# Layer 1's products on two column groups behind the sums over the values, with one shift in sixteen on GpSimd and a unit's last sums on TensorE

## The chip, the core and the metric

The kernel runs on one core of a Trainium2 chip. The metric is the device time of one execution in microseconds, lower is better. Before the change three executions took 4672.19, 4672.76 and 4673.68 us. A profiled execution, which all durations below come from, took 4667.5 us, with a span of 4665.7 us from the first to the last instruction and a mean granted TensorE clock of 0.997.

## The reference

The input x is two images of 256 channels and 64 x 64 = 4096 positions, in 32-bit floats. Two attention layers follow one another. Layer 0 normalises over the channels, has 4 heads of 16 channels, a gate and a sigmoid. The change leaves it alone. Layer 1 is this, with 4 heads of 64 channels:

```
qkv = einsum('oc,bchw->bohw', w_qkv, x) + b_qkv
q, k, v = split(qkv.reshape(b, 4, 3 * 64, 4096), 3, axis=2)
attn = softmax(einsum('bhdn,bhdm->bhnm', q, k) / 8, axis=-1)
out = einsum('bhnm,bhdm->bhnd', attn, v).reshape(b, 256, 64, 64)
return einsum('oc,bchw->bohw', w_out, out) + b_out + x
```

So for every image and head a matrix of 4096 x 4096 scores is formed, exponentials of it are taken, and it is multiplied with the values and divided by its row sums.

## The kernel before

**Units, groups, chunks and steps.** Layer 1 works in 32 units `(b, g, j)`: image b, pair of heads g, block j of 512 queries (eight blocks). A unit goes over the keys in 32 chunks of 128. A chunk is a tile of 128 keys x 2 heads x 512 queries, so 128 x 1024 numbers. The chunks of a unit fall into two groups of 16, each with its own maximum. The program is written as one loop over 16 steps a unit with two chunks a step, in the order in which each engine shall work (every instruction goes through `seq`, which keeps the order of the program on its engine). What belongs to a chunk is spread over several steps, with LAG = 11:

- `score(t)` (L865): for each of the two heads a product on TensorE of 64 rows x 128 columns, side by side on the two halves of the array's rows, into one of two "pair" buffers of PSUM (two banks each).
- `keep(t)` (L882): VectorE takes the running maximum of the group, `rmax` (L893); ScalarE copies the scores out of PSUM into a tile `raw` (L894). There are 26 `raw` buffers.
- At the end of a group, `turn_max` (L896) transposes the maxima on TensorE, once for each head, and `fold` (L911) reduces them on VectorE to the negated maximum of each query (L923). It is sent to memory and read back as a row, spread over all partitions (tile `row`, one buffer). `place_shift` (L939) copies the row to PSUM on ScalarE, in another order of its columns (L943).
- `shift(t)` (L949): 11 steps after its score, VectorE adds the negated maximum to the chunk (L951).
- `weigh(t)` (L958): ScalarE takes the exponential (L963); GpSimd adds the chunk to the group's running sum `acc` (L973 for a group's first two chunks, L975 for the others). In the last chunks of the last unit, TensorE does part of that work (`on_tensor`, `late_sums`).
- `gather(t)` (L996): TensorE multiplies the exponentials with the values and sums over the keys, for each head in one of two column groups of the array (128 rows x 64 columns, L1004). 16 chunks add up in PSUM; then ScalarE copies the sum out (L1015).
- After a unit: `total` (L1018) sums the two `acc` over the partitions on TensorE, in four column groups of 32 (L1026); `keep_total` copies them out (L1034) and sends them through memory, four stores and a load on SyncE's queue; `lose`, `add_sums`, `factors` join the two groups' sums (small operations on GpSimd, a reciprocal on VectorE, L1124); `turn_sums` (L1128, with `turned`, L1048) transposes the gathered sums, and `rows` (L1131) scales them on VectorE (L1135) and joins them on GpSimd (L1141, L1144).

**The products.** Next to this, TensorE makes the queries of the next unit, the keys and values for the unit eight units on, and in the last 8 units the output of the first image. Each is a block of 512 positions, cut into four quarters. `quarter` (L803) is a product of 128 rows x 128 columns over 256 positions (keys and queries, L806); `values_in` (L690) has two products of 128 rows x 128 columns over 128 columns of the weights (L693); `project_out` (L1156) is like a quarter (L1160). ScalarE copies the results out (`store_keys` L818, `store_values` L832, `keep_next_queries` L858, `output` L1170).

**The order.** `at(t, place, step)` hangs a piece of work on step t at a place. Within a step the loop at the end of the kernel runs in this order:

1. the scores of the step's two chunks; the exponential of the second chunk of the pair due one step before; pieces at "start"; pieces at "early";
2. `keep` of the first chunk; `shift` and `weigh` of the first chunk due now; pieces at "early end";
3. `keep` of the second chunk; `gather` of the two chunks of the pair due one step before; pieces at "late" and "late end";
4. `shift` of the second chunk due now; pieces at "end".

So on TensorE a piece "early" stands between the scores and the sums over the values (`gather`), and a piece "late" behind the sums and ahead of the next step's scores. On ScalarE "early end" stands ahead of the copy of the second chunk, and "start" behind the exponential and ahead of the copy of the first.

**PSUM.** Two "pair" buffers take four of the eight banks, the shifts two, `gather` one, and one bank called "misc" serves all else in turn: products, transposes and totals. Whoever wants "misc" waits until its last user was copied out.

Of the kernel before, what the change touches and what calls it, by code (L numbers as in the profile page):

```python
# [14 lines left out]
P = 128  # L15
# [11 lines left out]
def conv_attention_kernel(  # L27
# [738 lines left out]

    LATE = len(units) * NM - 2 * LAG
    with (
# [34 lines left out]
        def quarter(ps, xt, g, t, q):  # L803

            c, cols = q % 2, bass.ts(q // 2, NB // 2)
            seq(nc.tensor.matmul(  # L806
                ps[:, cols], w1[:, c, t, bass.ts(g, P)], xt[:, c, cols],
                start=(c == 0), stop=(c == CC - 1),
            ))

        def next_keys(b, g, i, q):
            if q == 0:
                halves_of["k"] = misc(f"k1p_{b}_{g}_{i}")
            quarter(halves_of["k"], loaded["kv", b, g, i], g, 1, q)
# [8 lines left out]
        def next_values(b, g, i, q):  # L823
            if q % 2 == 0:
                halves_of["vp"] = misc(f"v1p_{b}_{g}_{i}_{q}")
            values_in(halves_of["vp"], loaded["kv", b, g, i], g, q)
# [20 lines left out]
        def next_queries(u, q):  # L847
# [6 lines left out]
            quarter(halves_of["q"], loaded["q", u], g, 0, q)  # L854
# [84 lines left out]
        def place_shift(u, n):  # L939
# [7 lines left out]
            shifts[u, n] = ps  # L947

        def shift(t):  # L949
            u = units[t // NM]  # L950
            seq(nc.vector.tensor_tensor(  # L951
                raws[t], raws[t], shifts[u, t % NM // GS], ALU.add
            ))
# [4 lines left out]
        def weigh(t):  # L958
# [6 lines left out]
            if on_tensor(t):  # L965
                return
# [29 lines left out]
        def gather(t):  # L996
# [13 lines left out]
            elif t == 2 * END - 2:  # L1010
                late_sums((t, t + 1))
            raws.pop(t - 2, None)
# [5 lines left out]
        def total(u):  # L1018
# [3 lines left out]
            srows[u] = misc(f"sum1_{b}_{g}_{j}")  # L1022
            for n in range(NG):
                for k in range(2):
# [3 lines left out]
                        start=True, stop=True,  # L1028
# [127 lines left out]
        def project_out(b, j, o, q):  # L1156
            if q == 0 or o == 1 and q == 2:
                outs["ps"] = misc(f"o1_{b}_{j}_{o}_{q}")
            c, cols = q % 2, bass.ts(q // 2, NB // 2)
            seq(nc.tensor.matmul(  # L1160
                outs["ps"][:, cols], wo1[:, c, bass.ts(o, P)], loaded["ao", b, j][:, c, cols],
                start=(c == 0), stop=(c == CC - 1),
            ))
# [28 lines left out]

        for n, u in enumerate(units):
            b, g, j = u
            t0 = n * US
            if n > 0:
                at(t0 - 9, "start", lambda u=u, b=b, j=j: fetch(("q", u), x1[b][j]))
                for q in range(4):
                    at(t0 - (5, 5, 3, 2)[q], "early", lambda u=u, q=q: next_queries(u, q))
                at(t0 - 5, "early end", lambda u=u: keep_next_queries(u, 0))  # L1200
                at(t0 - 2, "early end", lambda u=u: keep_next_queries(u, 1))
            if n < len(units) - NJ:
                to = (*units[n + NJ][:2], j)
                at(max(t0 - 1, 0), "start", lambda to=to: fetch(("kv", *to), x1[to[0]][to[2]]))
                for q in range(4):
                    at(t0 + 2 + q, "early", lambda to=to, q=q: next_keys(*to, q))
                    at(t0 + (6, 7, 9, 10)[q], "early", lambda to=to, q=q: next_values(*to, q))
                at(t0 + 5, "early end", lambda to=to: store_keys(*to))
                for i, step in enumerate((t0 + 7, t0 + 10)):
                    at(step, "early end", lambda to=to, i=i: store_values(*to, i))  # L1210
# [12 lines left out]
            if u != units[-1]:  # L1223
                at(t1 + 4, "early", lambda u=u: total(u))
                at(t1 + 4, "early end", lambda u=u: keep_total(u))
                at(t1 + 1, "late", lambda u=u: lose(u))
                at(t1 + 5, "late end", lambda u=u: add_sums(u))
                at(t1 + 7, "start", lambda u=u: factors(u))
# [15 lines left out]
            if n >= len(units) - NJ:  # L1244
                b0 = B - 2
                at(t0 - 1, "start", lambda b0=b0, j=j: fetch_output(b0, j))
                for o in range(CC):
                    for q in range(4):
                        step = t0 + ((2, 3, 4, 5), (6, 7, 9, 10))[o][q]
                        at(step, "early", lambda b0=b0, j=j, o=o, q=q: project_out(b0, j, o, q))  # L1250
                at(t0 + 5, "early end", lambda b0=b0, j=j: output(b0, j, 0, 2))
                for part, step in enumerate((t0 + 7, t0 + 10)):
                    at(step, "early end", lambda b0=b0, j=j, part=part: output(b0, j, 1, part))
# [172 lines left out]
```

## Time and profile before

| | before |
|---|---|
| three executions, median | 4672.76 us |
| profiled execution: time, span | 4667.5 us, 4665.7 us |
| PE busy | 4496.5 us |
| DVE busy | 3894.2 us |
| ACT busy | 3429.5 us |
| POOL busy | 2513.9 us |
| layer 1's shift, L951 on DVE | 1024 times, 1209 ns each |
| layer 1's maximum, L893 on DVE | 960 times (and 32 first ones), 1217 ns each |
| GpSimd's sum, L975 and L973 on POOL | 883 times, 2373 ns each, and 64 times, 2385 ns each |
| scores, L876 on PE | 4096 records, 637 ns each |
| sums over the values, L1004 on PE | 4096 records, 605 ns each |
| totals, L1026 on PE | 248 records, 605 ns each |
| a quarter of a product, L806 on PE | records of 431 ns |

PE is TensorE's products, PEld its loads of weights, DVE VectorE, ACT ScalarE, POOL GpSimd, SP SyncE. A product in 32-bit floats leaves two records in the profile, and records of products that run side by side overlap; the busy time counts such time once. A line such as "L951 DVE ... xN | busy, mean" is a group of instructions of one line of the program. "x <- y: total, times, longest" in the table of waits says that x's engine stood idle until y was done. The timeline gives start, duration, engine, line and operation, with the idle time before it in brackets; like instructions that follow one another are drawn together (x8).

### The profile page before, as it was taken

The page shows a single profiled execution, that of the slowest core. Times are in us where ns is not written, and L with a number is a line of the kernel's source. Part 1 is how long each engine was busy: PE and PEld are TensorE (multiplying, and loading weights), DVE is VectorE, ACT ScalarE, POOL GpSimd, SP SyncE. Part 2 cuts the span into 40 slices and gives each one's busy share as a digit, 9 for nine tenths or more (in the row PEclk, how much of TensorE's full clock was granted, in tenths as well). Part 3 has the DMA queues.
Part 4 walks back from the last instruction along what each step waited for, and adds up shares of the span by engine and source line. Part 5 has one row for each costly group of instructions (what it writes and reads, how often), then busy time and mean ns, then how long its engine had stood idle before and what let it go on. Part 6 is the DMA issues. An engine that isn't in the chain of part 4 may idle for free. (4 is left out here: it accounts for less than half of the span.)

```text
span 4665.7 us, 70910 instructions
## 1 busy us (share of the span) xinstructions
PE 4496.5 (96%) x27290; PEld 1511.0 (32%) x27290; DVE 3894.2 (83%) x4506; ACT 3429.5 (74%) x4588; POOL 2513.9 (54%) x1306
## 2 busy tenths in 40 slices
PE   8999999999999999999999999999999999999998
PEld 3433333333333333332333333333333333222232
DVE  6777777777777777439999999999999999999997
ACT  3366666666666666668888888888888888888885
POOL 5300000000000000009999999999999999999995
PEclk9999999999999999999999999999999999999999
DMA  3100000000000000121111221111211112121213
GB/s 100 39 4 20 20 20 15 15 15 15 15 17 15 15 13 13 40 77 35 35 37 33 63 48 42 35 37 43 69 41 39 37 33 62 48 53 37 53 39 111
DMA packets 199682, 174.70 MB, mean 37 GB/s; under 512 B 121256, under 2 KB 122088, under 8 KB 199344
## 3 DMA queue, kind: packets, MB, share of 16 engines
q1 hardware_dynamic: 197488, 169.58, 13.9%
q8 instruction: 214, 3.51, 0.3%
q14 instruction: 124, 1.02, 0.1%
q10 hardware_dynamic: 1856, 0.59, 0.1%
HBM read 127.65 MB, written 42.48 MB: 36 GB/s over the span
## 5 line engine op out<-in xcount | busy, mean ns | idle before, releaser
L975 POOL TENSOR_TENSOR acc<-acc,raw 128x1024 f32<-128x1024 f32 x883 | 2095.2, 2373 | 82.3 <-ACT raw L963 21.1
L402 DVE TENSOR_REDUCE mx<-a 128x1 f32<-128x512 f32 x2048 | 1314.4, 685 | 449.7 <-PE a L398 448.7
L439 ACT ACTIVATE p<-s 128x512 f32<-128x512 f32 x2048 | 1107.8, 595 | 702.1 <-PE a L398 369.3
L876 PE MATMUL s<-q,k 64*128 64x512 f32 x4096 | 1120.9, 637 | 126.1 <-ACT raw L894 117.9
L951 DVE TENSOR_TENSOR raw<-raw,shift 128x1024 f32<-128x1024 f32 x1024 | 1234.2, 1209 | 3.9 <-ACT shift L943 2.6
L893 DVE TENSOR_TENSOR rmax<-s,rmax 128x1024 f32<-128x1024 f32 x960 | 1168.7, 1217 | 74.4 <-PE s L876 68.3
L436 PE MATMUL s<-q,kT 32*128 32x512 f32 x4096 | 1218.0, 640 | 0.0
L894 ACT COPY raw<-s 128x1024 f32<-128x1024 f32 x1024 | 1034.2, 1010 | 207.3 <-DVE rmax L893 162.0
L963 ACT ACTIVATE raw<-raw 128x1024 f32<-128x1024 f32 x1024 | 1084.8, 1060 | 133.6 <-DVE raw L951 101.2
L398 PE MATMUL a<-kT,q 32*128 32x512 f32 x4096 | 1129.3, 643 | 1.4 <-DVE mx L402 1.3
L1004 PE MATMUL av<-raw,v 128*64 128x512 f32 x4096 | 992.8, 605 | 3.5 <-ACT raw L963 3.4
L451 PE MATMUL av<-p,v 128*32 128x256 f32 (+1 forms) x7904 | 650.1, 399 | 0.6 <-ACT avs L465 0.6
L876 PEld LDWEIGHTS s<-q,k 64*128 64x128 f32 x4096 | 314.6, 185 | 858.5 <-ACT raw L894 600.9
L501 POOL TENSOR_TENSOR f<-f,dyn 128x16 f32<-128x16 f32 x15 | 3.3, 221 | 1027.3 <-DVE f L500 1027.3
L436 PEld LDWEIGHTS s<-q,kT 32*128 32x128 f32 x4096 | 397.2, 183 | 425.8 <-issue 392.6
L451 PEld LDWEIGHTS av<-p,v 128*32 128x32 f32 x7904 | 157.7, 108 | 751.4 <-issue 737.1
L1004 PEld LDWEIGHTS av<-raw,v 128*64 128x64 f32 x4096 | 247.7, 136 | 468.8 <-issue 350.1
L552 POOL TENSOR_SCALAR res<-res 128x1024 f32<-128x1024 f32 x16 | 16.7, 1045 | 659.6 <-ACT res L551 659.6
L398 PEld LDWEIGHTS a<-kT,q 32*128 32x128 f32 x4096 | 305.1, 183 | 31.5 <-DVE mx L402 18.2
L973 POOL TENSOR_TENSOR acc<-raw,raw 128x1024 f32<-128x1024 f32 x64 | 152.6, 2385 | 124.2 <-ACT raw L963 124.2
L923 DVE TENSOR_REDUCE negs<-rt 128x4 f32<-128x512 f32 x126 | 86.7, 688 | 50.4 <-PE rt L906 50.4
L306 DVE RECIPROCAL std<-std 128x128 f32<-128x128 f32 x64 | 56.1, 920 | 39.5 <-ACT std L301 39.5
(335 smaller groups left out, 1835.1 us busy)
## 6 DMA issues: line engine op xcount, KB each, us to landing
row<-neg SPq DMA_DIRECT2D x128, 256.0 KB
x<-in_x_dram SPq DMA_DIRECT2D x16, 512.0 KB
res<-in_x_dram SPq DMA_DIRECT2D x16, 512.0 KB
x<-res SPq DMA_DIRECT2D x16, 512.0 KB
att<-rows SPq DMA_DIRECT2D x62, 128.0 KB
kd<-k1s SPq DMA_DIRECT2D x24, 256.0 KB
vd<-v1s SPq DMA_DIRECT2D x24, 256.0 KB
k<-kd SPq DMA_DIRECT2D x24, 256.0 KB
```

Source lines behind the costliest of these rows:

```text
L398: seq(nc.tensor.matmul(ps, qs0[u][r, bass.ts(i, P)], kTs[b][r, bass.ts(m, NB)], start=True, stop=True,))
L402: seq(nc.vector.tensor_reduce(mxs[u][:, i * H + h, m : m + 1], ps, AX.X, ALU.max))
L436: seq(nc.tensor.matmul(ps, kTs[b][r, bass.ts(m, P)], qs0[u][r, :], start=True, stop=True))
L439: seq(nc.scalar.activation(pt[:, k, :], ps, AF.Exp, scale=D0**-0.5))
L451: seq(nc.tensor.matmul(avs[u][32 * h : 32 * h + 32, cols], vs0[b][:, m, 32 * h : 32 * h + 32], pts[t, h // 2][:, h % 2, cols], start=(m == ...
L876: seq(nc.tensor.matmul(ps[:, k, :], ks[b, g, m // PB][r, bass.ts(m % PB, P)], qs1[u][r, :], start=True, stop=True,))
L893: seq(nc.vector.tensor_tensor(rmax[u, n], ps, before, ALU.max))
L894: seq(nc.scalar.copy(raw, ps))
L951: seq(nc.vector.tensor_tensor(raws[t], raws[t], shifts[u, t % NM // GS], ALU.add))
L963: seq(nc.scalar.activation(p, p, AF.Exp, scale=D1**-0.5))
L975: seq(nc.gpsimd.tensor_tensor(accs[u, n], accs[u, n], p, ALU.add))
L1004: seq(nc.tensor.matmul(avs1[u, n][k * D1 : (k + 1) * D1, :], v[:, m % PB, k, :], raws[t][:, k, :], start=(m % GS == 0), stop=(m % GS == GS ...
```

## The change

Six things change, all in layer 1:

- `quarter` makes two products of 128 rows x 64 columns, one for each column group, in place of one of 128 x 128; so does `next_values` (its halves are 64 positions), and `project_out` now goes through `quarter`.
- These products, and `total`, hang "late" in place of "early". The copies of their results on ScalarE hang at the "start" of the next step in place of "early end" of the same. Two quarters of the queries move from step 11 to step 13, one from 13 to 14 (counted from the start of the unit before).
- For the chunk number 11 of each group (the twelfth), GpSimd adds the shift, straight from the tile `row`, right behind `place_shift`; VectorE leaves it out. The last group of the last unit keeps the old way.
- The last two chunks of each unit are no longer added to `acc` on GpSimd. Behind the last `gather` of a unit, TensorE sums them over the partitions, with four products of 128 x 32 columns into the bank of the total, and `total` adds the second group's `acc` onto them. So the "misc" bank belongs to the total from that step on.
- `add_sums` moves two steps later, and `factors` from the start of step 15 to the end of the step after.

```
--- before.py
+++ after.py
@@ -764,6 +764,9 @@
     END = len(units) * US
 
 
+    ALSO = 11
+
+
     LATE = len(units) * NM - 2 * LAG
     with (
         tc.tile_pool(name="l1", bufs=2) as l1,
@@ -800,18 +803,20 @@
 
 
 
-        def quarter(ps, xt, g, t, q):
+
+        def quarter(ps, xt, w, q):
 
             c, cols = q % 2, bass.ts(q // 2, NB // 2)
-            seq(nc.tensor.matmul(
-                ps[:, cols], w1[:, c, t, bass.ts(g, P)], xt[:, c, cols],
-                start=(c == 0), stop=(c == CC - 1),
-            ))
+            for k in range(2):
+                r = slice(k * D1, (k + 1) * D1)
+                seq(nc.tensor.matmul(
+                    ps[r, cols], w[:, c, r], xt[:, c, cols], start=(c == 0), stop=(c == CC - 1),
+                ))
 
         def next_keys(b, g, i, q):
             if q == 0:
                 halves_of["k"] = misc(f"k1p_{b}_{g}_{i}")
-            quarter(halves_of["k"], loaded["kv", b, g, i], g, 1, q)
+            quarter(halves_of["k"], loaded["kv", b, g, i], w1[:, :, 1, bass.ts(g, P)], q)
 
         def store_keys(b, g, i):
             k = l1.tile([P, NB], F32, tag="kv", name=f"k1s_{b}_{g}_{i}")
@@ -823,7 +828,14 @@
         def next_values(b, g, i, q):
             if q % 2 == 0:
                 halves_of["vp"] = misc(f"v1p_{b}_{g}_{i}_{q}")
-            values_in(halves_of["vp"], loaded["kv", b, g, i], g, q)
+            ps, xt = halves_of["vp"], loaded["kv", b, g, i]
+            for c in range(CC):
+                for k in range(2):
+                    r = slice(k * D1, (k + 1) * D1)
+                    seq(nc.tensor.matmul(
+                        ps[r, bass.ts(q, P)], xt[:, c, q * P + k * D1 : q * P + (k + 1) * D1],
+                        w1[:, c, 2, bass.ts(g, P)], start=(c == 0), stop=(c == CC - 1),
+                    ))
 
         def store_values(b, g, i, half):
             if half == 0:
@@ -851,7 +863,7 @@
                 qs1[u] = qt
             if q % 2 == 0:
                 halves_of["q"] = misc(f"q1p_{b}_{g}_{j}_{q}")
-            quarter(halves_of["q"], loaded["q", u], g, 0, q)
+            quarter(halves_of["q"], loaded["q", u], w1[:, :, 0, bass.ts(g, P)], q)
 
         def keep_next_queries(u, half):
             cols = bass.ts(half, NB // 2)
@@ -945,9 +957,19 @@
                 row.rearrange("p k (a m i) -> p (k a) i m", m=P, i=2),
             ))
             shifts[u, n] = ps
+            if (u, n) != (units[-1], NG - 1):
+                a = raws[units.index(u) * NM + n * GS + ALSO]
+                seq(nc.gpsimd.tensor_tensor(
+                    a.rearrange("p k (a i m) -> p (k a) i m", m=P, i=2),
+                    a.rearrange("p k (a i m) -> p (k a) i m", m=P, i=2),
+                    row.rearrange("p k (a m i) -> p (k a) i m", m=P, i=2),
+                    ALU.add,
+                ))
 
         def shift(t):
             u = units[t // NM]
+            if t % GS == ALSO and t < (len(units) - 1) * NM + GS:
+                return
             seq(nc.vector.tensor_tensor(
                 raws[t], raws[t], shifts[u, t % NM // GS], ALU.add
             ))
@@ -962,7 +984,7 @@
             p = raws[t]
             seq(nc.scalar.activation(p, p, AF.Exp, scale=D1**-0.5))
 
-            if on_tensor(t):
+            if on_tensor(t) or m >= NM - 2:
                 return
             if (u, n) not in first:
                 first[u, n] = p
@@ -1009,6 +1031,15 @@
                 late_sums((t - 1, t) if on_tensor(t - 1) else (None, t))
             elif t == 2 * END - 2:
                 late_sums((t, t + 1))
+            if m == NM - 1 and u != units[-1]:
+                srows[u] = misc(f"sum1_{b}_{g}_{j}")
+                for i in (t - 1, t):
+                    for k in range(2):
+                        r = D1 * (NG - 1) + 32 * k
+                        seq(nc.tensor.matmul(
+                            srows[u][r : r + 32, :], ones[:, :32], raws[i][:, k, :],
+                            start=(i < t), stop=False, skip_group_check=True,
+                        ))
             raws.pop(t - 2, None)
             if m % GS == GS - 1:
                 a = l1.tile([P, NB], F32, tag="avs", name=f"avs1_{b}_{g}_{j}_{n}")
@@ -1019,13 +1050,12 @@
 
 
             b, g, j = u
-            srows[u] = misc(f"sum1_{b}_{g}_{j}")
             for n in range(NG):
                 for k in range(2):
                     r = D1 * n + 32 * k
                     seq(nc.tensor.matmul(
                         srows[u][r : r + 32, :], ones[:, :32], accs[u, n][:, k, :],
-                        start=True, stop=True,
+                        start=(n < NG - 1), stop=True, skip_group_check=True,
                     ))
 
         def keep_total(u):
@@ -1156,11 +1186,7 @@
         def project_out(b, j, o, q):
             if q == 0 or o == 1 and q == 2:
                 outs["ps"] = misc(f"o1_{b}_{j}_{o}_{q}")
-            c, cols = q % 2, bass.ts(q // 2, NB // 2)
-            seq(nc.tensor.matmul(
-                outs["ps"][:, cols], wo1[:, c, bass.ts(o, P)], loaded["ao", b, j][:, c, cols],
-                start=(c == 0), stop=(c == CC - 1),
-            ))
+            quarter(outs["ps"], loaded["ao", b, j], wo1[:, :, bass.ts(o, P)], q)
 
         def output(b, j, o, part):
 
@@ -1190,24 +1216,25 @@
 
 
 
+
         for n, u in enumerate(units):
             b, g, j = u
             t0 = n * US
             if n > 0:
                 at(t0 - 9, "start", lambda u=u, b=b, j=j: fetch(("q", u), x1[b][j]))
                 for q in range(4):
-                    at(t0 - (5, 5, 3, 2)[q], "early", lambda u=u, q=q: next_queries(u, q))
-                at(t0 - 5, "early end", lambda u=u: keep_next_queries(u, 0))
-                at(t0 - 2, "early end", lambda u=u: keep_next_queries(u, 1))
+                    at(t0 - (3, 3, 2, 2)[q], "late", lambda u=u, q=q: next_queries(u, q))
+                at(t0 - 2, "start", lambda u=u: keep_next_queries(u, 0))
+                at(t0 - 1, "start", lambda u=u: keep_next_queries(u, 1))
             if n < len(units) - NJ:
                 to = (*units[n + NJ][:2], j)
                 at(max(t0 - 1, 0), "start", lambda to=to: fetch(("kv", *to), x1[to[0]][to[2]]))
                 for q in range(4):
-                    at(t0 + 2 + q, "early", lambda to=to, q=q: next_keys(*to, q))
-                    at(t0 + (6, 7, 9, 10)[q], "early", lambda to=to, q=q: next_values(*to, q))
-                at(t0 + 5, "early end", lambda to=to: store_keys(*to))
-                for i, step in enumerate((t0 + 7, t0 + 10)):
-                    at(step, "early end", lambda to=to, i=i: store_values(*to, i))
+                    at(t0 + 2 + q, "late", lambda to=to, q=q: next_keys(*to, q))
+                    at(t0 + (6, 7, 9, 10)[q], "late", lambda to=to, q=q: next_values(*to, q))
+                at(t0 + 6, "start", lambda to=to: store_keys(*to))
+                for i, step in enumerate((t0 + 8, t0 + 11)):
+                    at(step, "start", lambda to=to, i=i: store_values(*to, i))
 
                 t1 = (n // NJ * NJ + NJ - 1) * US
                 at(t1 + 2 * j + 2, "start", lambda to=to: load_keys(*to))
@@ -1221,11 +1248,11 @@
                 at(t1 + 2, "end", lambda u=u, k=k: place_shift(u, k))
             t1 = t0 + US + GS // 2
             if u != units[-1]:
-                at(t1 + 4, "early", lambda u=u: total(u))
-                at(t1 + 4, "early end", lambda u=u: keep_total(u))
+                at(t1 + 4, "late", lambda u=u: total(u))
+                at(t1 + 5, "start", lambda u=u: keep_total(u))
                 at(t1 + 1, "late", lambda u=u: lose(u))
-                at(t1 + 5, "late end", lambda u=u: add_sums(u))
-                at(t1 + 7, "start", lambda u=u: factors(u))
+                at(t1 + 7, "late end", lambda u=u: add_sums(u))
+                at(t1 + 8, "end", lambda u=u: factors(u))
                 for place, k in (("early", 1), ("late", 0)):
                     at(t1 + 9, place, lambda u=u, k=k: turn_sums(u, k))
                     at(t1 + 9, f"{place} end", lambda u=u, k=k: rows(u, k))
@@ -1247,10 +1274,10 @@
                 for o in range(CC):
                     for q in range(4):
                         step = t0 + ((2, 3, 4, 5), (6, 7, 9, 10))[o][q]
-                        at(step, "early", lambda b0=b0, j=j, o=o, q=q: project_out(b0, j, o, q))
-                at(t0 + 5, "early end", lambda b0=b0, j=j: output(b0, j, 0, 2))
-                for part, step in enumerate((t0 + 7, t0 + 10)):
-                    at(step, "early end", lambda b0=b0, j=j, part=part: output(b0, j, 1, part))
+                        at(step, "late", lambda b0=b0, j=j, o=o, q=q: project_out(b0, j, o, q))
+                at(t0 + 6, "start", lambda b0=b0, j=j: output(b0, j, 0, 2))
+                for part, step in enumerate((t0 + 8, t0 + 11)):
+                    at(step, "start", lambda b0=b0, j=j, part=part: output(b0, j, 1, part))
```

## The prediction

> **What bounds the kernel now.** I read the page first: does one engine bound the whole span? Its second view has PE at nine tenths everywhere, and DVE, ACT and POOL jump near the middle, where layer 1 begins. The page's totals mix two layers; the change touches layer 1 only, so I read 2500 to 4500 us of the table by windows (columns: PE, PEld, DVE, ACT, POOL busy).
>
> ```profile
> span 4665.7 us, 70910 instructions
> PE 4496.5 (96%) x27290; PEld 1511.0 (32%) x27290; DVE 3894.2 (83%) x4506; ACT 3429.5 (74%) x4588; POOL 2513.9 (54%) x1306
> ...
> 2500.00:4500.00 2000.00, 1897.26 (x7960) 613.92 (x7956) 1902.10 (x1753) 1741.69 (x1881) 1875.65 (x916) 1.00 0.19 46
> ```
>
> Three engines are at 94 to 95%, so none alone says what a step costs. The waits of the same stretch say who waits for whom:
>
> ```profile
> ACT raw L894 <- DVE rmax L893: 119.5, 202, 1.0
> PE s L876 <- ACT raw L894: 86.8, 174, 0.9
> POOL acc L973 <- ACT raw L963: 64.5, 51, 2.1
> DVE rmax L893 <- PE s L876: 52.1, 125, 0.6
> ```
>
> This is a ring: scores (PE), maximum (DVE), copy out of PSUM (ACT), next scores into the two freed "pair" buffers. The copies L1034, one per unit, stand 79.8 us apart (2182.1 to 4577.7 in 30 intervals: 79.85). I call a unit's 16 steps 0 to 15 and walk through one in the timeline. PE, steps 7 to 9 and 11 to 13:
>
> ```profile
> 3034.99 1.13 PE L876 MATMUL s<-q,k 64*128 64x512 f32 x4
> 3036.41 1.13 PE L876 MATMUL s<-q,k 64*128 64x512 f32 x4 [0.29 <-ACT raw L894]
> 3037.47 0.66 PE L906 MATMUL rt<-ident,rmax 128*128 128x128 f32 x4
> 3038.05 1.94 PE L1004 MATMUL av<-raw,v 128*64 128x512 f32 x8
> 3039.92 0.66 PE L906 MATMUL rt<-ident,rmax 128*128 128x128 f32 x4
> 3040.51 2.14 PE L876 MATMUL s<-q,k 64*128 64x512 f32 x8
> ...
> 3052.59 1.13 PE L806 MATMUL q1p<-b_('q', (0, 1, 5))_25110,w 128*128 128x256 f32 x4
> 3053.66 1.94 PE L1004 MATMUL av<-raw,v 128*64 128x512 f32 x8
> 3055.52 2.38 PE L876 MATMUL s<-q,k 64*128 64x512 f32 x8
> 3057.84 1.06 PE L1026 MATMUL sum<-acc,ones 128*32 128x512 f32 x8
> 3058.83 1.94 PE L1004 MATMUL av<-raw,v 128*64 128x512 f32 x8
> 3060.70 2.15 PE L876 MATMUL s<-q,k 64*128 64x512 f32 x8
> 3062.78 0.70 PE L806 MATMUL q1p<-b_('q', (0, 1, 5))_25110,w 128*128 128x256 f32 x2
> 3063.41 1.94 PE L1004 MATMUL av<-raw,v 128*64 128x512 f32 x8
> ```
>
> Starts count, since ends overlap. The second score waits for a copy; then everything follows in order. av takes 1.87 us, one product 0.63 (3062.78 to 3063.41), two in one go 1.07, so 0.44 each and 0.19 once for coming from and going to another shape. DVE spends 1.13 per rmax or shift from start to start (busy 1.21 overlaps), so 4.53 a step. From one rmax to the rmax of the same chunk parity two steps on: shift and second rmax 2.27 + 1.22, copy 0.08 + 1.01, second score 0.05 + 1.06, product 0.63, av 1.87, first score 1.18: **9.37 us for two steps**, 8.75 without a product; DVE alone needs 9.06. So the path changes between DVE and this ring. Followed back, with the first rmax of a step as marks, the unit divides into: step 3 to 9, 30.09 (3012.26 to 3042.35); on to the end of the second copy of step 10, 9.13; to step 13, 10.40; to 15, 9.37; to 1, 10.58; to 3, 10.24. Sum 79.81. Around step 8 DVE shows why:
>
> ```profile
> 3039.13 1.21 DVE L893 TENSOR_TENSOR rmax<-s,rmax 128x1024 f32<-128x1024 f32 x1
> 3040.61 0.69 DVE L923 TENSOR_REDUCE negs<-rt 128x4 f32<-128x512 f32 x1 [0.27 <-PE rt L906]
> 3041.22 1.21 DVE L951 TENSOR_TENSOR raw<-raw,shift 128x1024 f32<-128x1024 f32 x1
> 3042.35 1.22 DVE L893 TENSOR_TENSOR rmax<-s,rmax 128x1024 f32<-128x1024 f32 x1
> ```
>
> The scores for 3042.35 began at 3040.51 and could be used at 3040.51 + 1.18 = 3041.69: the shift before it costs 0.66.
>
> **What the Trainium skill says.** TensorEngine Tiling (Array Packing), Key Properties: changing the tiling mode drains TensorE, changing the tile does not. The trace agrees: 0.63 alone, 0.44 for the second. The same page, same section: tiles work in parallel; L1004's two column tiles do (605 ns a record, eight records in 1.87). SBUF — State Buffer, Who interferes with whom: a DVE instruction with one SBUF input doesn't contend with GpSimd; rmax and shift read one PSUM operand each and hold 1.21 us beside a busy POOL. GPSIMD Engine Reference, Performance pitfalls: reads with a step over 8 bytes cost about 50% more. The new shift reads a row with a step of two floats, 8 bytes, so at the edge; no row of before shows it on POOL.
>
> **The change part by part.**
> Products as 128*64 behind av. Each runs in the mode of av: 0.44 for 0.63 as lower cost. Upper cost: the two columns don't run beside each other, 0.88. I take 0.44 because L1004 shows the overlap for the same shape; the more numerous weight loads are short (PEld is a third busy). On the path lie one key product (step 4) and one value product (step 6): -0.38. The two query products of step 14 become 0.88 for 0.63: +0.25. The others are beside DVE.
> Evacuations a place later. The keys' activation stood on ACT before step 5's second copy: rmax ended at 3025.51, the copy could follow 0.08 later and began at 3025.94: -0.35. The values' copy now lies at step 8's start, behind an exponential, and the turned maxima need its one "misc" bank. From the end of step 7's second copy: 0.07 + exponential 1.06 + values' copy 0.35 = 1.5 us, where the scores alone take 0.05 + 1.06: **+0.40** in step 8. Who waits: everything behind the turn on PE, av too. The rest falls into ACT's gaps (13% idle).
> DVE loses 63 shifts, in steps 8 and 0 behind the second negs. Spacing 2 x 1.13 = 2.26 a unit, but the next rmax can gain only until its scores are there: -0.67 each (0.66 and 0.67), -1.34.
> POOL gains 63 shifts and loses 62 adds (two in each of 31 units). At the 2.43 us of an add this is nil; ends: 2.43, and 4.86 for twice, 3.65 for the skill's 50%. Its place matters: from L973 at the unit's first pair (start 3058.24) to the add of the 16th chunk POOL works 39.5 us, then 42.0; ACT's copy that reuses that chunk's buffer (26 buffers on, step 4) comes 42.2 after the same start (3020.67 + 79.81 - 3058.24); after the change the exponential of step 12, no longer behind a queries' copy and with the step's start earlier, comes some 1.5 sooner, that copy 0.94 sooner: 42.8. So nobody waits, with 0.8 to spare. The DMA of the row is there (ACT waits for it 1.1 us in all over the window). The row's single buffer is held a little longer, but the next is asked for six steps on.
> Last step's sums on TensorE: four 512-column products on two of four column groups, two behind each other: 2 x 0.87 (L1004's 1.87 holds two such) plus 0.11 of mode change = 1.85, in step 11, and queries leave it (1.07). The total stays 0.99, in step 12. From the copy of step 10: score, av, sums, two scores, av, total, score: 0.05 + 1.06 + 1.87 + 1.85 + 0.95 + 1.06 + 1.87 + 0.99 + 1.18 = 10.88 against 10.40: **+0.48**. Behind the sums wait the scores of step 12, and DVE for them.
> Moved sums and factors: total's four stores and one load on SP get two and a half steps before GpSimd's add, one and a half before; the reciprocal goes from step 15 to step 0's end, where DVE waits 0.47 anyway. If POOL were late with the factor, rows of step 1 would wait; it is due 0.5 to 1.9 us before. Nothing taken.
> Output products of the last 8 units change as keys and values do.
> Sum: step 3 to 9: -0.38 - 0.35 + 0.40 - 0.67 = -1.00; step 11 to 13 +0.48; 14 +0.25; step 0 -0.67: **-0.94 a unit**. POOL needs 79.8 less its waits 0.77 + 0.47 + 0.32 + 2.12 = 76.1, and 78.5 in the 8 output units (two more adds), so 78.9 is open to it. 31 units: -29 us. The profiled execution took 4667.5 us around its span of 4665.7; 4638 for it. The median shown, 4672.8, is 5.3 above: **4643**.
>
> **Rivals.**
> (B) Whole gain: the ring finds room and DVE's 2.26 count in full, until POOL binds: 23 x 2.26 + 8 x 1.33 = 62.6, **4610**. For it: DVE runs without a gap over whole steps. Against: it waits for scores 125 times.
> (C) Nothing: POOL's strided shift takes 3.65. Then output units cost 78.5 + 2.4 = 80.9, 8 x 1.1 lost, 23 units keep some 0.5: about **4669**. Also where the change's new waits (misc bank in step 8, POOL's factor) take all.
> (D) Slower: the two column halves of a product don't overlap, being short (256 or 128 columns) with a weight load each. Four products lie on the path (4, 6, two in 14): 4 x 0.44 more = +1.76 - 0.94 = +0.82, 31 units +25: **4698**. It decides from 0.675 us a product. For it: a 64-column load takes 136 ns, longer than a value record's stream (0.44 over four). Against: L1004.
>
> **How the numbers follow.** Forecast 0.47, B 0.18, C 0.16, D 0.19. The forecast's own range is 4625 to 4660 (a product at 0.40 to 0.55, sums 1.7 to 2.0). Over all, 4605 to 4686 takes in B and C and part of D. A measurement of this kernel can tell 0.2%, 9.3 us, from no change. Faster by more: forecast, B, little else, 0.65; within: C, 0.16; slower: D, 0.19.
>
> **What would show it.** Right: L1034 78.9 us apart; products 0.44 from start to start behind av; POOL's new row at 2.4 us; L951 961 times; more idle of DVE before rmax than 52 in the window; step 11 longest on PE. Wrong: products at 0.6 or more (D); POOL's row above 3 us and ACT's raw waiting for POOL (C); DVE gap-free at a unit of 77.5 (B).

## The result, and the profile after

| | before | after |
|---|---|---|
| median of 20 executions each | 4673.58 us | 4663.29 us |
| lowest and highest | 4671.24 and 4676.13 us | 4658.35 and 4670.88 us |
| profiled execution: time, span | 4667.5 us, 4665.7 us | 4664.3 us, 4662.5 us |
| mean distance of the totals' copies, one a unit | 79.85 us | 79.65 us |

The ratio is 0.9978, with an interval of [0.9971, 0.9985]: 10.3 us faster, where 30 had been forecast. The executions after lie 12.5 us apart, those before 4.9: a hint that something of varying length now stands on the path (in run 1 below, where that thing is taken off it, five executions lie 2.0 us apart).

First the page after: its head, the busy times, the groups of VectorE's shift and of GpSimd's new shift.

```profile
span 4662.5 us, 73152 instructions
PE 4499.5 (97%) x28490; PEld 1512.5 (32%) x28490; DVE 3833.0 (82%) x4443; ACT 3439.1 (74%) x4588; POOL 2514.5 (54%) x1307
...
L973 DVE TENSOR_TENSOR raw<-raw,shift 128x1024 f32<-128x1024 f32 x961 | 1160.5, 1212 | 26.9 <-ACT shift L955 26.9
...
L962 POOL TENSOR_TENSOR raw<-raw,row 128x1024 f32<-128x1024 f32 x63 | 152.0, 2412 | 37.3 <-ACT raw L906 37.1
```

The stretch from 2500 to 4500 us in the table by windows after (columns as before: PE, PEld, DVE, ACT, POOL busy):

```profile
2500.00:4500.00 2000.00, 1903.32 (x8928) 616.80 (x8926) 1857.50 (x1707) 1752.79 (x1884) 1877.55 (x917) 1.00 0.20 46
```

The change does what it says: 961 shifts on VectorE, 63 on GpSimd at 2.41 us. VectorE is less busy in the stretch (1857.5 us for 1902.1), the other three hardly differ. But in the shift's group the idle time is all put down to one thing, the copy of the row (26.9 us). The waits of the stretch follow it further (waiting engine and line, whom for, us in total, times, longest):

```profile
ACT raw L906 <- DVE rmax L905: 122.4, 177, 0.9
...
DVE rmax L905 <- PE s L888: 70.5, 152, 1.6
...
PE s L888 <- ACT raw L906: 67.5, 176, 0.7
POOL acc L995 <- ACT raw L985: 63.2, 26, 3.6
...
DVE raw L973 <- ACT shift L955: 20.1, 25, 1.4
PE av L1026 <- ACT raw L985: 19.5, 25, 1.4
...
ACT shift L955 <- DMA row<-neg: 19.3, 24, 1.4
```

The first four are the ring of before, with VectorE waiting 18 us more for scores. Among the new ones the last three belong together, and are of nearly the same size. Read from the last upwards: ScalarE's copy of the row waits for a DMA, VectorE's first shift of the new group waits for that copy, TensorE waits for the exponential behind that shift. The last line was 1.1 us in two times before; it is 19.3 us in 24 times now, 0.80 us on average, once in 24 of the stretch's 25 units (in the one left the copy stands 1.2 us as well, put down to VectorE). The timeline of ScalarE after shows how it enters a unit. These are two copies of totals, and the copies of the rows that follow them in step 2 of the next unit (start, duration, engine, line; idle time before in brackets):

```profile
2984.28 0.63 ACT L1064 COPY srow<-sum 128x512 f32<-128x512 f32 x1
...
3013.75 1.12 ACT L955 COPY shift<-row 128x1024 f32<-128x1024 f32 x1 [0.46 <-DMA row<-neg]
...
3063.58 0.64 ACT L1064 COPY srow<-sum 128x512 f32<-128x512 f32 x1
...
3093.51 1.11 ACT L955 COPY shift<-row 128x1024 f32<-128x1024 f32 x1 [0.92 <-DMA row<-neg]
```

The two totals stand 79.30 us apart, with a wait of 0.46 between them: 78.84 without it. In other units the distance and the wait are 79.11 and 0.27, 80.27 and 1.45, 79.05 and 0.21, 80.23 and 1.41: each leaves 78.82 to 78.84. (The last seven distances, of units with output products, leave 78.9 to 79.0.) So a unit after is **78.84 us plus its wait for the row**, and 78.84 is what the forecast had for a whole unit (78.87).

Why the row comes late is seen on SyncE's queue, around step 0 of the next unit. A group's two heads each send 2 KB of maxima to memory and read them back as 256 KB. After:

```profile
3079.47 0.36 SPq L938 DMA_DIRECT2D neg<-negs  x1
3082.86 0.34 SPq L942 DMA_DIRECT2D row<-neg  x1
3083.25 0.43 SPq L938 DMA_DIRECT2D neg<-negs  x1
3088.81 0.34 SPq L942 DMA_DIRECT2D row<-neg  x1
```

And the same four before, where nobody waited:

```profile
3078.35 0.36 SPq L926 DMA_DIRECT2D neg<-negs  x1
3081.37 0.34 SPq L930 DMA_DIRECT2D row<-neg  x1
3081.76 0.43 SPq L926 DMA_DIRECT2D neg<-negs  x1
3086.85 0.34 SPq L930 DMA_DIRECT2D row<-neg  x1
```

The end of the second fold (after, then before), and the copy that needs the row, before:

```profile
3081.21 0.69 DVE L935 TENSOR_REDUCE negs<-rt 128x4 f32<-128x512 f32 x1 [0.63 <-PE rt L918]
...
3080.09 0.69 DVE L923 TENSOR_REDUCE negs<-rt 128x4 f32<-128x512 f32 x1 [0.63 <-PE rt L906]
...
3092.18 1.11 ACT L943 COPY shift<-row 128x1024 f32<-128x1024 f32 x1
```

The order was bad already. After, the first head's load waits for its own store (3.4 us), and since SyncE takes one issue after the other, the second head's store stands behind it, though its data were ready at 3081.90. Its store then follows a load of 256 KB and takes 5.6 us until its own load can be issued; that load is used 4.7 us later. In sum 11.6 us from the second fold's end to the copy.

Before, the fold ended at 3080.78 and ScalarE was ready to copy at 3092.18: 11.4 us. There the load, issued at 3086.85, had landed by some 3091.55, if it took the 4.7 us of after: an estimated slack of 0.6 us. After, ScalarE is ready at 3093.51 - 0.92 = 3092.59, 10.7 us after the fold's end. The 0.7 us that went missing are the shift that the change took out from behind the second fold. By itself that is only 0.1 us more than the slack. The rest of the 0.92 us lies in the transfers: their second load is issued 6.9 us after the fold's end, not 6.1, because both stores took longer (3.4 and 5.6 us, not 3.0 and 5.1).

This is no accident of one unit. Over 30 units of each trace that load is issued 7.2 us after the second fold's end on average, before 6.7 (and 6.6 in the kernels of runs 2 and 3, where VectorE keeps its shift). After, the row is used 4.3 us behind the issue on average. With that length the row came some 0.4 us early before (11.4 - 6.7 - 4.3, an estimate): 0.7 from the shift and 0.5 from the transfers, less 0.4 of slack, make the 0.8 of wait. Why the same transfers took 0.5 us longer after, no run shows. **What the change gained in step 0 was lost again in step 2, waiting for a transfer.**

At the middle of a unit (step 8) both stores are issued first, and both loads after them; no wait shows there.

These DMAs carry no fixed place in this program: the code does not order them with `seq`, and their order on the queue came out differently at the two places.

VectorE around step 8 after, where the shift behind the second fold is gone as well:

```profile
3038.04 1.21 DVE L973 TENSOR_TENSOR raw<-raw,shift 128x1024 f32<-128x1024 f32 x1
3039.17 0.68 DVE L935 TENSOR_REDUCE negs<-rt 128x4 f32<-128x512 f32 x1
3039.77 1.22 DVE L905 TENSOR_TENSOR rmax<-s,rmax 128x1024 f32<-128x1024 f32 x1
3041.54 0.69 DVE L935 TENSOR_REDUCE negs<-rt 128x4 f32<-128x512 f32 x1 [0.56 <-PE rt L918]
3042.61 1.22 DVE L905 TENSOR_TENSOR rmax<-s,rmax 128x1024 f32<-128x1024 f32 x1 [0.38 <-PE s L888]
```

The last maximum now waits for its scores, 0.38 us, where a shift stood ahead of it before. So the gain was taken up to the scores' limit, as forecast.

### The profile page after: what moved, and what is told of

Its sections match the earlier page's. It is cut to its first block, busy times and chain, and to the rows that moved or that the text cites. A ratio compares the mean times of both kernels' runs of the same rounds, so it can differ in the third digit from the quotient of the medians.

```text
span 4662.5 us, 73152 instructions
## 1 busy us (share of the span) xinstructions
PE 4499.5 (97%) x28490; PEld 1512.5 (32%) x28490; DVE 3833.0 (82%) x4443; ACT 3439.1 (74%) x4588; POOL 2514.5 (54%) x1307
## 3 DMA queue, kind: packets, MB, share of 16 engines
q8 instruction: 223, 3.65, 0.3%
## 5 line engine op out<-in xcount | busy, mean ns | idle before, releaser
L997 POOL TENSOR_TENSOR acc<-acc,raw 128x1024 f32<-128x1024 f32 x821 | 1949.6, 2375 | 80.4 <-ACT raw L985 31.5
L973 DVE TENSOR_TENSOR raw<-raw,shift 128x1024 f32<-128x1024 f32 x961 | 1160.5, 1212 | 26.9 <-ACT shift L955 26.9
L1026 PE MATMUL av<-raw,v 128*64 128x512 f32 x4096 | 1005.9, 606 | 28.9 <-ACT raw L985 28.2
L962 POOL TENSOR_TENSOR raw<-raw,row 128x1024 f32<-128x1024 f32 x63 | 152.0, 2412 | 37.3 <-ACT raw L906 37.1
```

The lines of the kernel that those rows point to most:

```text
L973: seq(nc.vector.tensor_tensor(raws[t], raws[t], shifts[u, t % NM // GS], ALU.add))
L997: seq(nc.gpsimd.tensor_tensor(accs[u, n], accs[u, n], p, ALU.add))
L1026: seq(nc.tensor.matmul(avs1[u, n][k * D1 : (k + 1) * D1, :], v[:, m % PB, k, :], raws[t][:, k, :], start=(m % GS == 0), stop=(m % GS == GS ...
```

## The experiments

Theory R: the late row alone makes up the missing 19 us. Its rivals (with letters of their own, apart from the prediction's): V, the parts do not add up, because the relief of VectorE is eaten by the ring of scores; G, GpSimd holds the units, since it is busy 94% of the stretch; and H, the column halves save nothing. Every ratio is against the kernel before on the same chip. A "unit" is the distance of the totals' copies in the units ahead of those with output products.

**1. Both stores first, after and before.** The core of the edit, for both kernels (`fold`, called once for each head k):

```
-            nc.sync.dma_start(
+            seq(nc.sync.dma_start(
                 out=to.rearrange("o (a p i) -> p (o a) i", p=P, i=2),
...
-            nc.sync.dma_start(out=rows_in[u, n][:, k, :], in_=to.partition_broadcast(P))
+            if k == 1:
+                for i in range(2):
+                    seq(nc.sync.dma_start(
+                        out=rows_in[u, n][:, i, :],
+                        in_=neg1[u, n][i : i + 1, :].partition_broadcast(P),
+                    ))
```

> The changed kernel, where both heads' negated maxima are sent to memory before either row is read back. Row theory (what the forecast missed is the wait for the row at step 2, 0.83 us a unit): the wait of ACT's shift copy for the row falls below 0.1 us a unit, the totals' copies stand 78.85 us apart in place of 79.65, and the whole takes 31 x 0.8 = 25 us less than the changed kernel, 4638 us (0.9925 of before). GpSimd theory (the longer chain on GpSimd holds the rest): the row comes earlier but ACT's raw copy waits for GpSimd instead, and the time stays at 0.997 to 0.998.

> The kernel before with the same order of the transfers. Row theory: its row arrives about when it is needed (1.1 us of waits in 25 units), so nothing to gain: within 0.1% of before, and units still 79.8 us apart. If the order of the transfers is worth something by itself, it is faster by 10 us or more.

After: 4639.64 us beside 4667.93, ratio 0.9938 [0.9926, 0.9951], that is -28 us; units of 78.89. Before: 4667.01, ratio 0.9998 [0.9989, 1.0006]; units of 79.82. The same reordering is worth nothing to the kernel before. The kernel after it takes from 0.9978 to 0.9938, some 18 us, and so to nearly all of the forecast's gain. SyncE's queue in the reordered kernel after, at the same place of a unit:

```profile
3068.17 2.82 SPq L938 DMA_DIRECT2D neg<-negs  x2
3071.29 2.84 SPq L944 DMA_DIRECT2D row<-neg  x2
```

Drawn together are two stores (3068.17 and 3070.63), then two loads (3071.29 and 3073.79). The second load is issued 3.2 us after its fold's end at 3070.60, not 6.9. ScalarE's copy follows without a wait:

```profile
3080.27 1.01 ACT L906 COPY raw<-s 128x1024 f32<-128x1024 f32 x1
3081.35 1.12 ACT L960 COPY shift<-row 128x1024 f32<-128x1024 f32 x1
3082.39 1.06 ACT L990 ACTIVATE raw<-raw 128x1024 f32<-128x1024 f32 x1
```

R holds: the wait is gone from the table of waits, and the units are at 78.89. The Trainium skill describes why a store can stand behind another transfer's wait (DMA: Bandwidth & Descriptors, Anatomy of one DMA, in its account of GpSimd's path): a DMA's wait is taken by the sequencer that issues it, ahead of dispatch. The four lines of SyncE's queue after agree: 3.4 us between a store and the load that needs it, and the next store behind. The page's "~2.0 us" of fixed cost for a transfer (measured there on GpSimd's path) is less than these stores took in the units shown: 3.0 and 3.4 us alone, 5.1 and 5.6 behind a load.

**2. The products alone.** The kernel after without GpSimd's shift and without TensorE's sums of the last step; all shifts on VectorE, all sums on GpSimd.

```
-            if (u, n) != (units[-1], NG - 1):
-                a = raws[units.index(u) * NM + n * GS + ALSO]
-                seq(nc.gpsimd.tensor_tensor(
...
-            if t % GS == ALSO and t < (len(units) - 1) * NM + GS:
-                return
...
-            if on_tensor(t) or m >= NM - 2:
+            if on_tensor(t):
...
```

> Only the products on two column groups and all the moved places; all shifts on VectorE, all sums over the chunks on GpSimd. By the forecast's own terms: the products -0.38, the keys' copy -0.35, the misc bank's +0.40 hidden behind VectorE's shift in step 8, queries gone from step 11 -0.6, two in step 14 +0.25: -1.08 a unit, 33 us less than before, about 4640. The row is not late, since steps 0 to 2 keep their length. If the products' part gives nothing and the shift on GpSimd is what the changed kernel gains by, it stays within 5 us of before.

4662.32 us, ratio 0.9988 [0.9981, 0.9994], units of 79.60: a miss. The expectation had left the prediction's own sum aside. By its steps, products and places alone are -0.38 - 0.35 + 0.40 + 0.25 = -0.08 a unit; measured are -0.22. The products' move is worth little by itself.

**3. All shifts on VectorE again.** Only GpSimd's shift is undone; the sums of the last step stay on TensorE.

> The changed kernel with all shifts on VectorE again (GpSimd has two adds less in each unit and nothing in their place). Row theory: the shift behind the second fold comes back in steps 0 and 8, 0.66 each on 78.84, the row is no longer waited for: 80.2 a unit, 1.0023 of before, about 4685. GpSimd theory: GpSimd has 4.8 us more room in a unit, so it is faster than the changed kernel, below 0.997.

4681.96 us, ratio 1.0030 [1.0019, 1.0042], units of 80.27, and no wait for a row. The waits of its stretch:

```profile
POOL acc L985 <- ACT raw L975: 172.7, 50, 7.1
ACT raw L906 <- DVE rmax L905: 98.5, 175, 1.0
```

GpSimd is idle 172.7 us, up to 7.1 at a time, and the kernel is slower than before: G doesn't explain the kernel after. Against the products alone this kernel differs by the sums on TensorE: +0.67 a unit, where the forecast had +0.48. And where VectorE has its old load, no row is late: step 0 has its old length, and the second load is issued 6.6 us after the fold's end on average, not 7.2.

**4. The sums back on GpSimd.** Only TensorE's sums of the last step are undone; GpSimd keeps its shift.

```
-            if on_tensor(t) or m >= NM - 2:
+            if on_tensor(t):
...
-            if m == NM - 1 and u != units[-1]:
-                srows[u] = misc(f"sum1_{b}_{g}_{j}")
-                for i in (t - 1, t):
...
```

> The changed kernel with the last two chunks of each unit added on GpSimd again; the shift stays on GpSimd. GpSimd then has two operations of 2.43 us more in each unit: 76.1 + 4.9 = 81.0, and 83.4 in the eight units with outputs. If GpSimd bounds it: 23 x 1.2 + 8 x 3.5 = 56 us more than before, 1.012. If instead TensorE's sums in step 11 were what holds the changed kernel back, taking them away makes it faster than the changed kernel, 0.995 or less.

4710.69 us, ratio 1.0089 [1.0075, 1.0102], less than the 1.012 expected, but the same way; units of 80.7, and of 83.0 where the output products stand. Its waits:

```profile
ACT raw L906 <- POOL acc L997: 65.4, 52, 2.3
...
ACT raw L906 <- POOL acc L995: 14.6, 31, 1.0
```

Here GpSimd does bind: the copies that reuse its buffers wait. The sums on TensorE are the price of giving GpSimd a shift.

**5. Whole products in the new places.** The reordered kernel after, with products of 128 x 128 behind the sums over the values. The keys' and queries' part of the edit (the values go back to `values_in`):

```
-            for k in range(2):
-                r = slice(k * D1, (k + 1) * D1)
-                seq(nc.tensor.matmul(
-                    ps[r, cols], w[:, c, r], xt[:, c, cols], start=(c == 0), stop=(c == CC - 1),
-                ))
+            seq(nc.tensor.matmul(
+                ps[:, cols], w[:, c], xt[:, c, cols], start=(c == 0), stop=(c == CC - 1),
+            ))
```

> The changed kernel with both stores first, and the products again as one of 128 columns, in their new places. The forecast's terms: 0.63 in place of 0.43 for a first product and 0.44 for a second, so 0.19 in steps 4, 6 and 14: 0.6 a unit, 18 us over the kernel with stores first, some 0.998 of before. If column groups don't matter and only the places do: 0.994, as with column groups.

4661.57 us, ratio 0.9984 [0.9977, 0.9991], units of 79.56: the column groups are worth 0.67 us a unit, as expected. H falls.

**6. Shift and sums alone.** The kernel before with GpSimd's shift, the sums of the last step on TensorE and both stores first; the products, and the total's place, as before.

> The kernel before with the shift on GpSimd and the last sums on TensorE, products and copies in their old places, and both stores ahead of the rows, so that the row is not the question. Step 11 then holds two queries' products and the sums, 1.07 + 1.85: +1.5 between steps 11 and 13, against -0.67 in each of steps 8 and 0: about +0.2 a unit, within 0.3% of before. If the parts simply add up (whole with stores first 0.9938, products alone 0.9988), it is 0.995.

4689.45 us, ratio 1.0044 [1.0031, 1.0056], units of 80.56: a miss, and a strong one. TensorE and VectorE at step 11:

```profile
3059.78 1.13 PE L807 MATMUL q1p<-b_('q', (0, 1, 5))_25133,w 128*128 128x256 f32 x4
3060.84 1.94 PE L1020 MATMUL av<-raw,v 128*64 128x512 f32 x8
3063.06 1.91 PE L1033 MATMUL sum<-raw,ones 128*32 128x512 f32 x8 [0.28 <-ACT q L859]
3064.90 1.99 PE L877 MATMUL s<-q,k 64*128 64x512 f32 x8
```

```profile
3062.25 1.21 DVE L967 TENSOR_TENSOR raw<-raw,shift 128x1024 f32<-128x1024 f32 x1
3066.07 1.23 DVE L894 TENSOR_TENSOR rmax<-s,rmax 128x1024 f32<-128x1024 f32 x1 [2.61 <-PE s L877]
```

Two query products are still ahead of the sums over the values in this step, and the sums need the "misc" bank that those fill, so TensorE waits for their copy as well. VectorE stands 2.61 us, against 1.55 us in the kernel after. So the move of the products makes room for the sums. It need not be all: ScalarE's copies also wait for GpSimd here, 39.9 us in 89 times over the stretch (17.7 us in 26 times in the kernel after), and `add_sums` and `factors` have their old places. The two shares were not taken apart.

**7. One sum instead of two.** The reordered kernel after; in the 24 units without output products TensorE sums only the last chunk, and GpSimd adds the other.

```
+        def last_sums(u):
+            return 1 if units.index(u) < len(units) - NJ else 2
...
-            if on_tensor(t) or m >= NM - 2:
+            if on_tensor(t) or m >= NM - last_sums(u):
...
-                for i in (t - 1, t):
+                for i in range(t + 1 - last_sums(u), t + 1):
```

> The changed kernel with both stores first; in the 24 units without outputs TensorE sums only the last chunk and GpSimd adds the one before it. TensorE loses 0.87 in step 11, and steps 11 to 13 set the end there: unit down to 78.0 by that, but GpSimd comes to 76.1 + 2.4 = 78.5. So 0.4 in 23 units, 9 us less than with both sums on TensorE: 0.992. If GpSimd's chain up to step 4 already binds, no gain or a loss.

4632.44 us, ratio **0.9922 [0.9908, 0.9935]**, the fastest that computes everything: 0.48 us less in each of these units (78.41). GpSimd had room for the add there: in the reordered kernel it waits 59.3 us for exponentials ahead of its sums over the stretch, 2.4 us a unit, and an add takes 2.4. Now it has hardly any left: where the output products begin, one unit takes 83.21 us, with a copy of ScalarE that waits 2.24 us for an add.

**8. Does VectorE's load hold the gain?** Theory V asks whether the removed shifts count in full. Three kernels, all with both stores first: the products alone as a control, and two in which the shift of the twelfth chunk is left out and not made up, so that nothing of its cost moves to GpSimd or TensorE.

```
             u = units[t // NM]
+            if t % GS == ALSO and t < (len(units) - 1) * NM + GS:
+                return
             seq(nc.vector.tensor_tensor(
```

> The column-group products in their new places alone (no shift on GpSimd, no sums of the last step on TensorE), with both stores of a group's maxima ahead of both row loads. Control for the next kernel: with all shifts on VectorE no row was late but twice, so units of 79.60 us as without the reordering, ratio 0.999. If the late row took the gain of the products too, 79.4 or less.

> As the control, but VectorE leaves the shift of the twelfth chunk out and nobody makes it up (that part of the computation is left out). If VectorE's load is what held the products' gain, units of 78.3 us or less (79.60 less the 1.34 a unit that the prediction gave to the removed shifts, or more), ratio about 0.990. If the ring through TensorE holds the units, 79.3 or more, ratio 0.997 or more.

> The kernel before with both stores first, VectorE leaving the shift of the twelfth chunk out (that part of the computation is left out), products in their old places and shapes. If the parts add up: 79.82 less 1.34, 78.5 us a unit, ratio 0.991. If the removed shifts and the new products need each other (the old products hold the ring where VectorE is relieved), 79.2 or more, ratio 0.996 or more.

They took 4661.02 us (0.9986 [0.9980, 0.9993]), 4618.45 us (0.9895 [0.9878, 0.9911]) and 4631.14 us (0.9922 [0.9907, 0.9937]). With their units, and those of runs 1 and 6, all with both stores first:

| unit, us | all as it was | shift left out | GpSimd's shift, sums on TensorE |
|---|---|---|---|
| products in old places | 79.82 | 78.56 | 80.56 |
| products in new places, column groups | 79.59 | 78.20 | 78.89 |

The removed shifts are worth 1.26 and 1.39 us a unit, where the forecast had 1.34, whatever the products do: V falls. What depends on the places is the price of getting rid of the shift: +2.00 in the old ones, +0.69 in the new ones (with `add_sums` and `factors` moved too).

## Why the prediction was wrong

It had the direction right, and the other steps right in kind; a wait that it put at nothing took most of the gain. By its own steps, on the unit from 3013 to 3093 us of the trace after, and by the runs:

| step of the prediction | forecast | found |
|---|---|---|
| shifts off VectorE, steps 8 and 0 | -1.34 | -1.26 and -1.39 (run 8) |
| column groups for whole products: -0.38, and 0.88 for 1.07 in step 14 | -0.57 | -0.67 (run 5) |
| step 3 to 9, without the row's wait | -1.00 | -1.16 |
| sums of the last step, step 11 to 13 | +0.48 | +0.63 in the trace, +0.67 and +0.69 in runs 3 and 8 |
| two queries in step 14 | +0.25 | +0.24 |
| step 0 | -0.67 | -0.66 |
| waits for the row | 0 | **+0.80** |

The lines of TensorE after, at steps 7, 8, 11 and 14, carry most of it:

```profile
3033.42 1.94 PE L1026 MATMUL av<-raw,v 128*64 128x512 f32 x8
3035.19 0.61 PE L835 MATMUL v1p<-w,xb_('kv', 1, 0, 4)_25090 128*64 128x128 f32 x8
3035.72 1.13 PE L888 MATMUL s<-q,k 64*128 64x512 f32 x4
...
3038.39 0.66 PE L918 MATMUL rt<-ident,rmax 128*128 128x128 f32 x4 [0.25 <-ACT v1s L844]
...
3052.84 2.18 PE L1026 MATMUL av<-raw,v 128*64 128x512 f32 x8
3054.95 1.91 PE L1039 MATMUL sum<-raw,ones 128*32 128x512 f32 x8
3056.79 1.99 PE L888 MATMUL s<-q,k 64*128 64x512 f32 x8
...
3065.44 1.03 PE L812 MATMUL q1p<-b_('q', (0, 1, 5))_25331,w 128*64 128x256 f32 x8
3066.40 2.12 PE L888 MATMUL s<-q,k 64*128 64x512 f32 x8
```

- **Column groups: right.** Two queries take 0.96 us from start to start, 0.48 each. One value product and the sums over the values ahead of it come to 0.43 more than those sums alone: 3033.42 to 3035.72 is 2.30 us, against 1.87.
- **Misc bank in step 8: right in kind, smaller.** The turn waits 0.25 us for the values' copy; 0.40 was forecast. The 0.15 us between the two would account for nearly all of the 0.16 by which step 3 to 9 came out better than forecast.
- **Sums of the last step: right in kind, some 30 to 45% dearer.** The four products take 1.84 us from start to start, 1.85 forecast. A difference shows in the sums over the values ahead of them, which take 2.11 us here (3052.84 to 3054.95), not 1.87.
- **GpSimd's strided shift: right.** 2.41 us, against 2.375 for its add. The Trainium skill's 50% for a step of over 8 bytes (GPSIMD Engine Reference, Performance pitfalls for Q7 kernels) does not set in at the row's 8 bytes.
- **"So nobody waits" for GpSimd: wrong, at no cost.** ScalarE's copies wait for an add of GpSimd, 17.7 us in 26 times over the stretch, 19 of them in step 1 of a unit and mostly for 0.75 us. The same copy stood 0.75 us in the trace before (at 3086.01), put down to VectorE's maximum. In the unit taken apart here, the stretch from step 15 to step 1 came out at 9.92 us, as forecast (9.91), and step 1 to 3 at 10.25 (10.24).
- **The step that failed** is the sentence "The DMA of the row is there (ACT waits for it 1.1 us in all over the window)". A wait of nearly nothing was read as proof of room. It only says that the row came in time, not by how much: the slack was some 0.4 us on average, 0.6 in the unit shown (estimates). The same text took 0.67 us out of step 0, between the fold that feeds the row and the copy that needs it, and never set the one against the other. Another half microsecond of the wait came from the transfers themselves, which took longer after; this could not be read from the trace before. The list of what is late next named scores, the misc bank and GpSimd; it should have named this transfer, whose four issues and the time from the last issue to the use stand in the trace of before.

In sum the unit's other terms came to 78.84 where 78.87 was forecast, and the wait put 0.80 back. Of the forecast's -0.94 a unit -0.2 was left in the profiled executions. The medians lie further apart than the spans of these (10.3 and 3.2 us), because the profiled execution before, 4667.5 us, was 6 us below its median. Run 1 gives the counterproof: without the wait, -28 us against the -29 us that the prediction's sum had for 31 units. That the two are so close is in part luck: the sums' price was underestimated by 0.15 us a unit and the misc bank's overestimated by as much.

Rival C's time (4669) came nearest, but for reasons that do not hold: GpSimd's strided add is not 3.65 us, and neither the misc bank nor GpSimd's factor took the gain. Rival D is refuted by run 5, rival B by run 8: of the 2.26 us that VectorE no longer works in a unit, 1.26 to 1.39 are gained even where nobody makes the shift up.

What stays open: why the stores took longer after than before; how TensorE and GpSimd share the price in run 6; why one head's store is issued behind the other head's load at a unit's end and not in its middle. Where the last 0.15 to 0.2 us of the sums' price come from was read in one unit and not tried by itself.

## What to carry to other kernels

Before you shorten a stretch of the critical path, list the transfers that start ahead of it and are used behind it, and work out for each by how much it comes early: a transfer without a wait may have half a microsecond of slack, and half a microsecond is also what its length may change by. Where a small store and a load that depends on it go through one queue, issue all stores ahead of all such loads, for the loads' waits hold up whatever stands behind them. And take the price of a move apart: here the shift was worth the same everywhere, and what decided was its price, which fell from 2.00 to 0.69 us once other work had been moved out of the way.

## What the runs showed of the hardware

- A store of 2 KB let the load that depended on it be issued after 3.0 and 3.4 us in the units shown, and after 5.1 and 5.6 us where it stood right behind a load of 256 KB on the same queue. Over 30 units of each trace the first took 2.7 to 4.3 us (means 3.2 before, 3.4 after), the second 4.2 to 7.3 us (5.6 and 5.9). So the chain for a second head was 11.6 us long, and 3.7 us shorter to its load's issue with the stores first, with the same bytes moved.
- Products of 128 x 64 on two column groups over only 128 columns, with eight weight loads for eight records, took 0.43 us behind the sums over the values, no longer than the queries' products over 256 columns (0.48 each). The weight loads did not make them longer, though a value product has twice as many of them.
